# LayerNorm folded into the q and k weights of a gated cross-attention kernel

## The chip, the cores and the metric

The kernel runs on one core of a Trainium2 chip. Its time is the device time of the whole program in microseconds (us). The core has a matrix engine (TensorE, PE in the profile, with its weight loads as PEld), VectorE (DVE), ScalarE (ACT), GpSimd (POOL) and SyncE (SP), which here issues the transfers. Each engine works through its own instructions in order; semaphores tie them together. Lines such as L518 are lines of the kernel before.

## What is computed

The input x is 8 batches of 512 rows by 2048 columns; the context ctx has the same shape. LayerNorm runs along the 2048 columns, so each batch has one mean and one reciprocal deviation for each of its 512 rows.

```python
x = x + tanh(g_xattn) * xattn(layernorm(x), ctx, mask, ...)
x = x + tanh(g_ffn)   * ffn(layernorm(x), ...)

# xattn, on patches of 128 columns, 8 heads of 32 rows
q = Wq @ qk + bq          # Wq, Wk: 256 x 512; qk = layernorm(x)
k = Wk @ qk + bk
val = Wv @ ctx + bv
o = softmax(q^T k / sqrt(32), masked) applied to val
out = (Wo @ gelu(o) + bo) * mask

# ffn, on x as 4 streams of 512 columns
H = sinkhorn(50 iterations on a 4 x 4 matrix per row, from x_norm @ W_res)
out = H mixed over the streams + (H_pre-weighted sum @ W_branch) spread by H_post
```

## The kernel before

The work is cut into 32 blocks of 512 columns, four to a batch, and each block into four steps t, one for each patch of 128 columns. A block of x is held as four tiles of 128 rows by 512 columns (xt). The pool of these tiles has 16 buffers, four blocks.

For block n, `proj(n)` makes q and k. POOL normalizes each of the four tiles (xn, L500), ACT casts it to float16 (xh, L505), and POOL takes the rest as a second float16 tile (xl, L507). The 512 output rows, q and k together, come in four groups m of 128. For each m and each tile, TensorE adds three float16 products in PSUM (L518 to L520): high weights by high x, high weights by low x, low weights by high x. ACT adds the bias and writes the float16 high part (ev, L522), and DVE the low part (L523). SP sends both to a scratch tensor (qd), from where `stack` fetches them into the layout QS and KS of the attention products.

A batch's mean and reciprocal deviation come from `stats(b)`, some blocks earlier: products of transposed x with the ffn weights (lgx, L448; rawp, L467), then squares of x on ACT (xs, L481), then `finish_stats`.

The rest of a step: `vproj` projects the context (vp, L559, float32), `smax` and `expo` form the scores twice (L569, L595), `attv` applies them (u, L612 and L616), and `outp` makes the output rows once per block: POOL multiplies by the mask (o, L632), TensorE transposes (gTp, L641), and four groups of products (op, L667 to L670) are added into xt by DVE (L671). SP stores xt to a scratch tensor (x1s, L674). After a batch, `ffn` runs the Sinkhorn iterations as a chain of small DVE instructions (L844 to L854), and `mixv` mixes the streams (w, L946 and L949 on DVE, L925 and L944 on POOL). Part of the mixing is done by TensorE at the end (`mixp`, L1000 and L1001).

What is emitted in a step follows the string `ORDER`, one letter for one kind of work; a scheduler with a simulated timeline then fixes the order on each engine. During block n, `proj(n + 2)` is run in parts, and in its last step the tiles of x for block n + 3 are requested:

```python
if LXP == 4 and p == 3 and n > 0 and n + 3 < NTOT:
    defer(D_LX, "lx", lambda n=n: load_x(n + 3))
```

The PSUM pool `ps_p`, with two buffers, serves proj, vproj and outp; `ps_t`, with two, serves most small products.

Of the kernel before, what the change touches and what calls it, by code (L numbers as in the profile page):

```python
# [9 lines left out]
F32 = mybir.dt.float32  # L10
# [9 lines left out]
P = 128  # L20
# [5 lines left out]
BLK = 512  # L26
# [9 lines left out]
CT_ACT = False  # L36
MH_ACT = False
XS_ACT = False
LXP = 4
POOLMIX = lambda i, j: j == 1 and i > 0  # L40
BUF_GP = 1
BUF_OP = 1
BUF_XHP = 5
BUF_XNP = 2
BUF_XTP = 4
BUF_CTP = 2
BUF_QDP = 3
# [17 lines left out]
BUF_XPRE = 1  # L65
PSTEPS = (0,1,1,2)
SP0 = 1
XH_POOL = lambda c: False
CAP = 1.0
NORM0 = True  # L70
D_MH = 0
# [1 line left out]
D_X1 = 0  # L73
D_OUT = 0
D_ST = 0
D_LX = 0
CT_PRE = False
BUF_XP = 16
PE_MIX = ((), (), (), (), (3,), (0, 1, 2, 3), (0, 1, 2, 3), (1, 2, 3))
SPLITS = (1, 1, 1, 1, 1, 1, 1, 1)  # L80
CHAINS = ((0,), (1,), (2,), (3,), (4,), (5,), (6,), (7,))
# [18 lines left out]
def gated_xattn_mhc_kernel(  # L100
# [43 lines left out]
    onesb = ctile([P, P], F32, "onesb")  # L144
    V.memset(onesb, 1.0)

    WqkH = ctile([P, 4, 512], F16, "WqkH")
    WqkL = ctile([P, 4, 512], F16, "WqkL")
# [25 lines left out]
    mrow_d = dram.tile([6, B * S], BF16, tag="mrow_d", name="mrow_d")  # L174
    mneg_d = dram.tile([1, B * S], F16, tag="mneg_d", name="mneg_d")
    brow_d = dram.tile([3, 512], F32, tag="brow_d", name="brow_d")


    QS = [ctile([99, NH, SB], F16, f"QS{i}") for i in range(NS)]
# [6 lines left out]
    xnp = ctx.enter_context(tc.tile_pool(name="xnp", bufs=BUF_XNP))  # L186
# [32 lines left out]
    rawx = {}  # L219
    nmean = {}  # L220
    rstd1 = {}
    nb1 = {}
    sq2 = {}
    x1s = {}
    G4 = {}
# [24 lines left out]

    def finish_stats(b, nm, var):
        r = rsqrt(ln0, var, eps_ln, 4, "ln1")
        nb = ln0.tile([P, 4], F32, tag="nb1", name="nb1")
        V.tensor_tensor(nb, nm, r, ALU.mult)
        nmean[b], rstd1[b], nb1[b] = nm, r, nb

    with tc.tile_pool(name="set", bufs=1) as st:

# [66 lines left out]
        for t in range(2):  # L325
            sl = slice(256 * t, 256 * t + 256)
            V.tensor_scalar(wq[:, :, sl], wq[:, :, sl], al[:, t : t + 1], None, ALU.mult)
        A.copy(WqkH, wq)
        V.tensor_tensor(WqkL, wq, WqkH, ALU.subtract)
        for t in range(2):  # L330
            V.tensor_scalar(bqs[:, 2 * t : 2 * t + 2], bcol[:, 2 * t : 2 * t + 2], al[:, t : t + 1], None, ALU.mult)

# [10 lines left out]
        var0 = stile([P, 4], F32, "var0")  # L343
        V.tensor_copy(var0, mv[:, :, 1])
        finish_stats(0, nm, var0)


        mh = stile([B * 16, 3, P], BF16, "mh")
# [91 lines left out]
    def stats(b):  # L440

        lgs = xsp.tile([P, 512], F32, tag="lgs", name="lgs", bufs=1)
        for q4 in range(5):
            if q4 > 0:
                flush(lambda e: e[2] == "st")
                lg = ps_t.tile([P, 512], F32, tag="t", name="lgx")
                for g in range(4):
                    T.matmul(lg[32 * g : 32 * g + 32, :], Wm[:, 4 * q4 - 4 + g, :], xts[g], start=True, stop=True)  # L448
                if q4 == 1:
                    V.tensor_copy(lgs, lg)  # L450
                else:
                    V.tensor_tensor(lgs, lg, lgs, ALU.add)
# [12 lines left out]
        rp = ps_t.tile([P, 4, 32], F32, tag="t", name="rawp")  # L465
        for c in range(4):
            T.matmul(rp[:, c, :], lgs[:, c * P : (c + 1) * P], sel, start=True, stop=True)  # L467
        rw = lnp.tile([P, 4, 32], F32, tag="rawx", name="rawx")
        V.tensor_copy(rw, rp)
        rawx[b] = rw  # L470
        if b == 0:
            return
        nm = ln0.tile([P, 4], F32, tag="nmean", name="nmean")
        V.tensor_scalar(nm, rw[:, :, NM], -1.0 / S, None, ALU.mult)
        yield 1
        sq = lnp.tile([P, 4, NBLK], F32, tag="sq1", name="sq1")
        for c in range(4):
            for k in range(NBLK):
                xs = xtp.tile([P, BLK], F32, tag="xTt", name="xs")
# [12 lines left out]
    def proj(n):  # L492

        b, k = divmod(n, NBLK)
        flush(lambda e: e[2] == "lx")
        xt = xtile[n]
        hs, ls = [], []
        for c in range(4):
            xn = xnp.tile([P, BLK], F32, tag="xn", name="xn")
            G.tensor_scalar(xn, xt[c], rstd1[b][:, c : c + 1], nb1[b][:, c : c + 1], ALU.mult, ALU.add)  # L500
            h = xhp.tile([P, BLK], F16, tag="xh", name="xh")
            if XH_POOL(c):
                G.tensor_copy(h, xn)
            else:
                A.copy(h, xn)  # L505
            l = xhp.tile([P, BLK], F16, tag="xl", name="xl")
            G.tensor_tensor(l, xn, h, ALU.subtract)  # L507
            hs.append(h)
            ls.append(l)
        if NORM0:  # L510
            yield
        qd = qdp.tile([2, 4, 2, P, BLK], F16, tag="qd", name="qd")
        qds[n] = qd
        for m in range(4):
            ps = ps_p.tile([P, BLK], F32, tag="p", name="qk")
            ms = slice(m * P, (m + 1) * P)
            for c in range(4):
                T.matmul(ps, WqkH[:, c, ms], hs[c], start=(c == 0), stop=False)  # L518
                T.matmul(ps, WqkH[:, c, ms], ls[c], start=False, stop=False)  # L519
                T.matmul(ps, WqkL[:, c, ms], hs[c], start=False, stop=(c == 3))  # L520
            ev = evp.tile([P, 2, BLK], F16, tag="ev", name="ev")
            A.activation(ev[:, 0, :], ps, AF.Identity, bias=bqs[:, m : m + 1])  # L522
            V.scalar_tensor_tensor(ev[:, 1, :], ps, bqs[:, m : m + 1], ev[:, 0, :], ALU.add, ALU.subtract)  # L523
            defer(D_QD, "qd", lambda m=m, ev=ev: SY.dma_start(qd[m // 2, 0:2, m % 2].rearrange("t p s -> p t s"), ev))
            yield

    def stack(m):
# [484 lines left out]
            pass  # L1012

    run(proj(0))
    stack(0)
    vproj(0)
    for t in range(2):
# [29 lines left out]
    def act(c, t):  # L1047
# [18 lines left out]
            if p == 2:  # L1066
                at("stack", stack, NSB * (n + 1) + 1)
        elif c == "l" and live_:
            if LXP == 4 and p == 3 and n > 0 and n + 3 < NTOT:
                defer(D_LX, "lx", lambda n=n: load_x(n + 3))  # L1070
            if LXP == 5 and p == 2 and n > 0 and n + 3 < NTOT:
                defer(D_LX, "lx", lambda n=n: load_x(n + 3))
            if p == LXP and n > 1 and n + 2 < NTOT:
                defer(D_LX, "lx", lambda n=n: load_x(n + 2))
# [121 lines left out]
```

## Time and profile before

| | |
|---|---|
| median of 3 runs | 1835.11 us (1830.48 to 1844.21) |
| profiled execution, its own time | 1828.05 us |
| its span, first to last instruction | 1825.9 us |
| busy: PE / PEld / DVE / ACT / POOL | 1547 / 901 / 1382 / 1069 / 603 us |
| mean granted TensorE clock | 0.932 of full speed |
| bytes moved | 331 MB, 181 GB/s over the span |

A line of a group reads: line, engine, operation, output and inputs by the program's names, shapes, count, then busy time in us and the mean ns of one, then the idle time of the engine just before, with what ended it. In the waits, the three numbers are the total in us, how often, and the longest. A line of one source line's instructions gives minimum, median and maximum in ns. Matmuls are pipelined, and the ends shown for them are modelled: they overlap, and two starts lie closer together than one duration.

### The profile page before, as it was taken

The numbers are of one execution on the slowest core, as the hardware profiler recorded it, in microseconds if no ns is written. First come the engines' busy times: TensorE is split into PE (matmuls) and PEld (weight loads), VectorE is DVE, ScalarE is ACT, GpSimd is POOL, SyncE is SP. The second block draws the span as 40 slices with busy tenths as digits, with TensorE's granted clock in tenths as the row PEclk, the third lists the DMA queues.
The fourth block names the chain that finished last, engine by engine and source line by source line (L and its number), as shares of the span: only waits on it lengthen the run. The fifth ranks groups of instructions, "written<-read, shape, count | busy, mean of one in ns | idle before, by whom it ended". The sixth has DMA issues, their size and how long they took to land.

```text
span 1825.9 us, 32268 instructions
## 1 busy us (share of the span) xinstructions
PE 1547.1 (85%) x10517; PEld 901.0 (49%) x10517; DVE 1382.3 (76%) x4201; ACT 1069.4 (59%) x2030; POOL 602.8 (33%) x511
## 2 busy tenths in 40 slices
PE   3998999989889888889878888799888889768887
PEld 2554555555555554545544445455455555543333
DVE  7434345877888778888888879889898998998761
ACT  2386466646555656558565475566665566755454
POOL 0512222322232243342444333444334442321121
PEclk7999999999999988999988999899999999989999
DMA  6478696467646855568555784468755565523443
GB/s 214 139 209 256 208 258 194 140 174 232 180 134 200 254 169 165 151 192 269 162 154 164 214 251 144 139 196 259 215 154 165 148 189 147 172 93 119 144 157 117
DMA packets 353237, 330.60 MB, mean 181 GB/s; under 512 B 53351, under 2 KB 251303, under 8 KB 353070
## 3 DMA queue, kind: packets, MB, share of 16 engines
q1 hardware_dynamic: 353070, 328.55, 60.6%
q8 instruction: 83, 1.36, 0.3%
q14 instruction: 84, 0.69, 0.1%
HBM read 226.71 MB, written 101.16 MB: 180 GB/s over the span
## 4 chain that ended last, share of the span: by engine, by line
PE 37%; DVE 23%; DMA 18%; issue 9%; ACT 9%; POOL 4%; SPq 1%; ACTq 0%; POOLq 0%; DVEq 0%
PE vp L559 5%; DVE w L946 4%; DMA xs<-in_x_dram 4%; PE qk L518 3%; PE qk L519 3%; DMA out_dram<-w 3%; PE qk L520 3%; DMA x<-x1s 2%; PE mx L1000 2%; DMA x1s<-xt 2%; PE lgx L448 2%; DVE mx L571 2%; PE op L667 2%; DVE W L844 2%; PE mx L1001 2%
## 5 line engine op out<-in xcount | busy, mean ns | idle before, releaser
L559 PE MATMUL vp<-Wv,ct 128*128 128x256 f32 x1024 | 272.4, 418 | 16.7 <-DMA ct<-in_cx_dram 15.1
L500 POOL TENSOR_SCALAR xn<-xt,ln_r,nb 128x512 f32<-128x512 f32 x128 | 105.5, 826 | 501.2 <-DMA xt<-in_x_dram 385.7
L559 PEld LDWEIGHTS vp<-Wv,ct 128*128 128x128 f32 x1024 | 207.4, 210 | 68.0 <-issue 18.6
L518 PE MATMUL qk<-xh,WqkH 128*128 128x512 f16 x512 | 199.2, 390 | 29.4 <-ACT xh L505 16.3
L946 DVE SCALAR_TENSOR_TENSOR w<-x,Et,w 128x512 f32<-128x512 f32 x180 | 180.0, 1001 | 49.6 <-POOL w L944 34.0
L519 PE MATMUL qk<-xl,WqkH 128*128 128x512 f16 x512 | 197.9, 387 | 4.3 <-POOL xl L507 4.0
L520 PE MATMUL qk<-xh,WqkL 128*128 128x512 f16 x512 | 197.6, 386 | 0.0
L571 DVE TENSOR_REDUCE mx<-smax 128x8 f32<-128x1024 f32 x128 | 154.9, 1210 | 41.7 <-PE smax L569 41.3
L507 POOL TENSOR_TENSOR xl<-xn,xh 128x512 f16<-128x512 f32 x128 | 156.3, 1228 | 76.0 <-ACT xh L505 70.4
L597 ACT ACTIVATE e<-sT,ebi,esc 128x1024 f32<-128x1024 f32 x128 | 153.4, 1198 | 18.0 <-PE sT L595 17.9
L523 DVE SCALAR_TENSOR_TENSOR ev<-qk,bqs,ev 128x512 f16<-128x512 f32 x128 | 94.5, 739 | 77.5 <-ACT ev L522 76.1
L667 PE MATMUL op<-gh,WoH 128*128 128x512 f32 x256 | 120.9, 474 | 35.3 <-DVE ev L523 31.1
L944 POOL TENSOR_TENSOR w<-w,pj 128x512 f32<-128x512 f32 x60 | 80.1, 1334 | 213.1 <-ACT w L939 113.7
L505 ACT CAST xh<-xn 128x512 f16<-128x512 f32 x128 | 78.3, 612 | 103.7 <-POOL xn L500 102.9
L522 ACT ACTIVATE ev<-qk,bqs 128x512 f16<-128x512 f32 x128 | 86.9, 679 | 85.0 <-PE qk L520 78.7
L673 ACT ACTIVATE junk<-xt,nmean 128x512 bf16<-128x512 f32 x128 | 91.6, 716 | 73.9 <-DVE xt L671 41.3
L850 DVE TENSOR_TENSOR W<-E,uv 128x64 f32<-128x64 f32 x392 | 119.4, 307 | 5.4
L844 DVE TENSOR_TENSOR W<-E,uv 128x64 f32<-128x64 f32 x352 | 117.1, 335 | 4.8
L612 PE MATMUL u<-e,onesb 128*32 128x256 f32 x1024 | 102.7, 403 | 10.5 <-DVE mq L573 3.8
L668 PE MATMUL op<-gl,WoH 128*128 128x512 f32 x256 | 107.1, 418 | 0.0
L669 PE MATMUL op<-gh,WoL 128*128 128x512 f32 x256 | 106.6, 417 | 0.0
L632 POOL TENSOR_TENSOR o<-o,mb 128x1024 f32<-128x1024 f32 x32 | 75.6, 2364 | 93.2 <-ACT o L627 85.9
(287 smaller groups left out, 3504.6 us busy)
## 6 DMA issues: line engine op xcount, KB each, us to landing
xt<-in_x_dram SPq DMA_DIRECT2D x128, 256.0 KB
ct<-in_cx_dram SPq DMA_DIRECT2D x128, 256.0 KB
xTt<-in_xT_dram SPq DMA_DIRECT2D x128, 256.0 KB
qd<-ev SPq DMA_DIRECT2D x128, 256.0 KB
x1s<-xt SPq DMA_DIRECT2D x128, 256.0 KB
xs<-in_x_dram SPq DMA_DIRECT2D x112, 256.0 KB
QS<-qd SPq DMA_DIRECT2D x192, 128.0 KB
KS<-qd SPq DMA_DIRECT2D x192, 128.0 KB
```

The lines of the kernel that those rows point to most:

```text
L507: G.tensor_tensor(l, xn, h, ALU.subtract)
L518: T.matmul(ps, WqkH[:, c, ms], hs[c], start=(c == 0), stop=False)
L519: T.matmul(ps, WqkH[:, c, ms], ls[c], start=False, stop=False)
L520: T.matmul(ps, WqkL[:, c, ms], hs[c], start=False, stop=(c == 3))
L559: T.matmul(ps[:, h, :], ct[:, c, :], Wv[:, c, :], start=(c == 0), stop=(c == 3))
L571: V.tensor_reduce(mx, sc, AX.X, ALU.max)
L597: A.activation(e32, sc, AF.Exp, bias=ebi[:, t : t + 1], scale=esc[:, t : t + 1])
L667: T.matmul(ps, WoH[:, e, cs], gh[:, e], start=(e == 0), stop=False)
L668: T.matmul(ps, WoH[:, e, cs], gl[:, e], start=False, stop=False)
L844: V.tensor_tensor(W4[:, h], E4[:, h], vb[:, h], ALU.mult)
L850: V.tensor_tensor(W4[:, h], E4[:, h], ub[:, h], ALU.mult)
L946: V.scalar_tensor_tensor(w, x1[j], E[:, n, 4 * j + i : 4 * j + i + 1], w, ALU.mult, ALU.add)
```

## The change

The normalization of x goes out of `proj`. The weights of q and k, scaled as before, are kept in float32 in a scratch tensor (wqk_d). For each batch and each m, the new function `weights` loads 128 of their columns, multiplies the rows by the batch's reciprocal deviation on POOL, and makes the bias of q or k from the product of these weights with the negative mean. `proj` then multiplies x itself, in float32, by these weights: four matmuls for each m. Weights for m = 0 and 1 of a batch are made at the end of its `stats`, those for m = 2 and 3 in the projection of the last block of the batch before. The pool of x has 20 buffers in place of 16, and block n + 4 is requested where block n + 3 was.

```diff
-BUF_XHP = 5
-BUF_XNP = 2
+BUF_XHP = 1
+BUF_WQ = 6
-BUF_XP = 16
+BUF_XP = 20
...
     def finish_stats(b, nm, var):
         r = rsqrt(ln0, var, eps_ln, 4, "ln1")
-        nb = ln0.tile([P, 4], F32, tag="nb1", name="nb1")
-        V.tensor_tensor(nb, nm, r, ALU.mult)
-        nmean[b], rstd1[b], nb1[b] = nm, r, nb
+        nmean[b], rstd1[b] = nm, r
+
+    def weights(b, m, src=None):
+        w = wqp.tile([P, 4, P], F32, tag="wq", name="wqb")
+        if src is None:
+            SY.dma_start(w, wqk_d[m])
+            src = w
+        for c in range(4):
+            G.tensor_scalar(w[:, c], src[:, c], rstd1[b][:, c : c + 1], None, ALU.mult)
+        bp = ps_t.tile([P, BLK], F32, tag="t", name="bp")[:, 0:1]
+        for c in range(4):
+            T.matmul(bp, w[:, c], nmean[b][:, c : c + 1], start=(c == 0), stop=(c == 3))
+        bi = ln0.tile([P, 1], F32, tag=f"bi{m}", name="bi")
+        V.tensor_tensor(bi, bp, bqs[:, m : m + 1], ALU.add)
+        wqb[b, m] = (w, bi)
...
-        A.copy(WqkH, wq)
-        V.tensor_tensor(WqkL, wq, WqkH, ALU.subtract)
+        for m in range(4):
+            SY.dma_start(wqk_d[m], wq[:, :, m * P : (m + 1) * P])
...
         finish_stats(0, nm, var0)
+        for m in range(4):
+            weights(0, m, wq[:, :, m * P : (m + 1) * P])
...
         finish_stats(b, nm, var)
+        for m in range(2):
+            weights(b, m)
...
     def proj(n):
         b, k = divmod(n, NBLK)
-        flush(lambda e: e[2] == "lx")
         xt = xtile[n]
-        hs, ls = [], []
-        for c in range(4):
-            xn = xnp.tile([P, BLK], F32, tag="xn", name="xn")
-            G.tensor_scalar(xn, xt[c], rstd1[b][:, c : c + 1], nb1[b][:, c : c + 1], ALU.mult, ALU.add)
-            h = xhp.tile([P, BLK], F16, tag="xh", name="xh")
...
-                A.copy(h, xn)
-            l = xhp.tile([P, BLK], F16, tag="xl", name="xl")
-            G.tensor_tensor(l, xn, h, ALU.subtract)
...
         for m in range(4):
             ps = ps_p.tile([P, BLK], F32, tag="p", name="qk")
-            ms = slice(m * P, (m + 1) * P)
+            if (b, m) not in wqb:
+                weights(b, m)
+            w, bi = wqb[b, m]
             for c in range(4):
-                T.matmul(ps, WqkH[:, c, ms], hs[c], start=(c == 0), stop=False)
-                T.matmul(ps, WqkH[:, c, ms], ls[c], start=False, stop=False)
-                T.matmul(ps, WqkL[:, c, ms], hs[c], start=False, stop=(c == 3))
+                T.matmul(ps, w[:, c], xt[c], start=(c == 0), stop=(c == 3))
             ev = evp.tile([P, 2, BLK], F16, tag="ev", name="ev")
-            A.activation(ev[:, 0, :], ps, AF.Identity, bias=bqs[:, m : m + 1])
-            V.scalar_tensor_tensor(ev[:, 1, :], ps, bqs[:, m : m + 1], ev[:, 0, :], ALU.add, ALU.subtract)
+            A.activation(ev[:, 0, :], ps, AF.Identity, bias=bi)
+            V.scalar_tensor_tensor(ev[:, 1, :], ps, bi, ev[:, 0, :], ALU.add, ALU.subtract)
             defer(D_QD, "qd", ...)
+            if k == NBLK - 1 and m < 2 and (b + 1, 1) in wqb:
+                weights(b + 1, m + 2)
             yield
...
     run(proj(0))
+    load_x(NBLK)
...
-            if LXP == 4 and p == 3 and n > 0 and n + 3 < NTOT:
-                defer(D_LX, "lx", lambda n=n: load_x(n + 3))
+            if p == 3 and n > 0 and n + 4 < NTOT:
+                load_x(n + 4)
```

More of the change, by code (lines that the diff above doesn't have):

```diff
@@ L38 @@
 XS_ACT = False
-LXP = 4
 POOLMIX = lambda i, j: j == 1 and i > 0
@@ L67 @@
 SP0 = 1
-XH_POOL = lambda c: False
 CAP = 1.0
@@ L75 @@
 D_ST = 0
-D_LX = 0
 CT_PRE = False
-BUF_XP = 16
+BUF_XP = 20
 PE_MIX = ((), (), (), (), (3,), (0, 1, 2, 3), (0, 1, 2, 3), (1, 2, 3))
@@ L145, in gated_xattn_mhc_kernel @@
     V.memset(onesb, 1.0)
-    WqkH = ctile([P, 4, 512], F16, "WqkH")
-    WqkL = ctile([P, 4, 512], F16, "WqkL")
     Wv = ctile([P, 4, DK], F32, "Wv")
@@ L176, in gated_xattn_mhc_kernel @@
     brow_d = dram.tile([3, 512], F32, tag="brow_d", name="brow_d")
+    wqk_d = dram.tile([4, P, 4, P], F32, tag="wqk_d", name="wqk_d")
     QS = [ctile([99, NH, SB], F16, f"QS{i}") for i in range(NS)]
@@ L185, in gated_xattn_mhc_kernel @@
     xsp = ctx.enter_context(tc.tile_pool(name="xsp", bufs=2))
-    xnp = ctx.enter_context(tc.tile_pool(name="xnp", bufs=BUF_XNP))
+    wqp = ctx.enter_context(tc.tile_pool(name="wqp", bufs=BUF_WQ))
     xhp = ctx.enter_context(tc.tile_pool(name="xhp", bufs=BUF_XHP))
@@ L221, in gated_xattn_mhc_kernel @@
     rstd1 = {}
-    nb1 = {}
+    wqb = {}
     sq2 = {}
@@ L494, in proj @@
         b, k = divmod(n, NBLK)
-        flush(lambda e: e[2] == "lx")
         xt = xtile[n]
-        hs, ls = [], []
-        for c in range(4):
-            xn = xnp.tile([P, BLK], F32, tag="xn", name="xn")
-            G.tensor_scalar(xn, xt[c], rstd1[b][:, c : c + 1], nb1[b][:, c : c + 1], ALU.mult, ALU.add)
-            h = xhp.tile([P, BLK], F16, tag="xh", name="xh")
[L502 to L505, printed above, removed]
-            l = xhp.tile([P, BLK], F16, tag="xl", name="xl")
-            G.tensor_tensor(l, xn, h, ALU.subtract)
-            hs.append(h)
-            ls.append(l)
         if NORM0:
@@ L1068, in act @@
         elif c == "l" and live_:
-            if LXP == 4 and p == 3 and n > 0 and n + 3 < NTOT:
-                defer(D_LX, "lx", lambda n=n: load_x(n + 3))
[L1071 to L1074, printed above, removed]
+            if p == 3 and n > 0 and n + 4 < NTOT:
+                load_x(n + 4)
         elif c == "s" and live_ and t + AHEAD < NT_:
```

## The prediction

> **What bounds the kernel now.** I read the page's busy shares first, then the table by stage, then the order of single matmuls on TensorE.
>
> ```profile
> PE 1547.1 (85%) x10517; PEld 901.0 (49%) x10517; DVE 1382.3 (76%) x4201; ACT 1069.4 (59%) x2030; POOL 602.8 (33%) x511
> ```
> PE has the largest share, but an average hides stages. The table by stage (columns: length, then busy time of PE, PEld, DVE, ACT, POOL, the granted TensorE clock, DMA share, GB/s) separates them:
>
> ```profile
> 60.00:350.00 290.00, 268.89 (x2001) 159.26 (x1999) 131.05 (x296) 177.55 (x336) 85.97 (x76) 0.98 0.73 212
> 350.00:650.00 300.00, 271.04 (x2051) 165.82 (x2052) 244.55 (x759) 176.62 (x360) 86.85 (x77) 0.97 0.65 193
> 650.00:950.00 300.00, 245.91 (x1704) 149.80 (x1704) 247.86 (x702) 182.13 (x348) 121.81 (x97) 0.91 0.63 184
> 950.00:1250.00 300.00, 252.69 (x1791) 149.21 (x1791) 253.69 (x728) 176.34 (x334) 109.70 (x90) 0.90 0.61 183
> 1250.00:1550.00 300.00, 258.33 (x1863) 159.98 (x1862) 267.18 (x801) 193.32 (x370) 128.39 (x104) 0.93 0.62 181
> ```
> Up to 650 us PE is busy 93% and 90%: this stage is TensorE's. From 650 us on, PE (82 to 86%) and DVE (83 to 89%) share the limit, and the clock is lower. The chain that ended last agrees that no engine rules alone:
>
> ```profile
> PE 37%; DVE 23%; DMA 18%; issue 9%; ACT 9%; POOL 4%; SPq 1%; ACTq 0%; POOLq 0%; DVEq 0%
> ```
> A block (512 columns of one batch; 32 of them) takes about 48 us: some 1540 us from 60 to 1600, divided by 32. The last 226 us hold no projection and are left alone by the change.
>
> **PE: the projection.** The timeline of PE shows the price of both forms side by side (start, duration, instruction):
>
> ```profile
> 63.74 3.62 PE L559 MATMUL vp<-Wv,ct 128*128 128x256 f32 x16
> 67.19 0.38 PE L518 MATMUL qk<-xh,WqkH 128*128 128x512 f16 x1
> 67.41 0.38 PE L519 MATMUL qk<-xl,WqkH 128*128 128x512 f16 x1
> 67.62 0.38 PE L520 MATMUL qk<-xh,WqkL 128*128 128x512 f16 x1
> ```
> Durations (0.38) overlap, so I take distances between starts. Float16: 0.215 us for 512 columns. Float32: the 16 records are 8 matmuls (two records each) of 256 columns and take 67.19 - 63.74 = 3.45 us, 0.431 each, so 0.862 for 512 columns: four times float16. One m of the projection was 12 float16 matmuls, 12 x 0.2155 = 2.59 us, and becomes 4 float32 ones, 4 x 0.862 = 3.45 us. With 32 blocks x 4 m = 128: 331 us become 442 us, **+110 us**. Fewer instructions, more time.
>
> Here a rule speaks differently. The Trainium skill, Perfetto Trace Analysis, "Identifying the Most-Contended Engine", calls matmul busy time a bad measure of TensorE and points to the busy share of weight loads instead (with FLOP utilization). That share is 49%, and the change moves it little: 1536 float16 loads x 0.099 = 152 us go, 1024 x 0.19 = 195 us of float32 loads come. By that rule half of TensorE is free and the +110 us cost nearly nothing; by the distances above the array is occupied without a gap inside each group, and they cost in full wherever PE sets the pace. I take the distances.
>
> **PE: the bias products.** 32 calls (4 m x 8 batches) of 4 float32 matmuls with one column, each with a full float32 weight load. Nearest row, the same load with 32 columns, 8 groups of 4:
>
> ```profile
> L467 PE MATMUL rawp<-sel,lgs 128*128 128x32 f32 x64 | 9.4, 288 | 4.1 <-DVE lgs L452 4.1
> ```
> 9.4 / 8 = 1.18 us per group, **+38 us**. Lower end 0.6 us per call (half of the loads hidden under the matmul before): 19 us. Upper end: PE is in order and waits for POOL's scaling, which may stand behind one 2.4 us POOL operation (o L632, gl L657): 3 us more for each of 28 calls, +84; queued behind on PE are smax, sT and u. It also borrows one of the two PSUM buffers of "t". The products of a batch are issued about a block ahead of their use, so I take 38.
>
> **POOL and ACT.** Removed per block: 4 xn, 4 xl, 4 xh.
>
> ```profile
> L500 POOL TENSOR_SCALAR xn<-xt,ln_r,nb 128x512 f32<-128x512 f32 x128 | 105.5, 826 | 501.2 <-DMA xt<-in_x_dram 385.7 <-DVE nb L254 71.3 <-DVE W L844 20.2
> L507 POOL TENSOR_TENSOR xl<-xn,xh 128x512 f16<-128x512 f32 x128 | 156.3, 1228 | 76.0 <-ACT xh L505 70.4 <-DVE mq L573 1.4 <-DVE W L850 1.2
> L505 ACT CAST xh<-xn 128x512 f16<-128x512 f32 x128 | 78.3, 612 | 103.7 <-POOL xn L500 102.9
> ```
> 262 us of POOL and 78 us of ACT go. Added on POOL: 128 scalings of 128x128; between the 0.21 us of a 128x4 copy (L635) and the 0.77 median of L500, by width 0.35 us, 45 us in all. POOL falls from 603 to 386 us. Neither engine is a bound, so the direct gain is only what PE waited for.
>
> ```profile
> PE op L667 <- DVE ev L523: 31.1, 21, 4.9
> ...
> PE qk L518 <- ACT xh L505: 16.3, 13, 4.7
> ...
> PE qk L518 <- DVE ev L523: 10.7, 7, 3.6
> ...
> PE qk L519 <- POOL xl L507: 4.0, 7, 1.3
> ```
> The waits for xh and xl, 20 us, go with their producers. The two for ev are waits for a PSUM buffer of the projection to be emptied by ACT and DVE (0.68 + 0.74 us); with 3.45 instead of 2.59 us of matmuls between two of them, I take half, 21 us. Together **-41 us** (ends -20 and -62). What is late next is the same DVE eviction, and DVE's gT (18 us), which stay.
>
> **DVE behind POOL.** The second rule, and it speaks for the change: SBUF — State Buffer, "Who interferes with whom", says that a VectorE instruction with two SBUF inputs and a GpSimd instruction that reads SBUF exclude each other, the later one blocking fully. The trace agrees in kind:
>
> ```profile
> L946 DVE SCALAR_TENSOR_TENSOR w<-x,Et,w x180: 647/746/2962, 510.4 to 1821.4; 128x512 f32<-128x512 f32 x180
> L850 DVE TENSOR_TENSOR W<-E,uv x392: 154/224/2371, 329.1 to 1766.4; 128x64 f32<-128x64 f32 x196
> ```
> Mean minus median, times count: L946 (1001-746) x 180 = 46 us; L850 33; L844 39; mq L573 and L574 32; L860 and L861 7: 157 us of blocked DVE. POOL loses 36% of its work, so 56 us of it. Read as a bound by the rule, DVE and the time gain 56; by the chain, of which DVE is 23%, 13 (below nothing there is no reason to go: nothing is added to DVE but 32 tiny adds). DVE is a co-limit in the later stage, so I take **-20**.
>
> **Clock.** Later stages are granted 0.90 to 0.93, the first 0.98. Fewer gaps on PE may raise it: at most 5% of 757 us of PE work, 38; lower end 0; I take **-10**.
>
> **x tiles and queues.** load_x(n+4) stands where load_x(n+3) stood. With 20 tiles it reuses block n-1's, as before with 16: SP still waits for that block's x1s store (104 us in total, 76 times), so SP is not freed; x merely arrives a block earlier. POOL's 386 us of waiting for xt cost nothing, as POOL was idle; what reached PE is in the 16.3 us already. SP gets 32 more transfers (4 stores, 28 loads of 256 KB, some 0.45 us of issue each) under 1540 us of body; bytes rise by 8.4 MB on 331. The loads of m = 2, 3 wait for a weight buffer that PE is still reading: at most 3.45 us x 14 = 48 us of SP standing, with ct, qd and QS/KS behind it; I take 0, as those loads are issued ahead. Without that cover it costs the 48. In the prologue wbr, which shares wq's space, now waits for the 16 scalings (about 43 to 48 us instead of 41), and PE for its product; PE then has 14 us of proj(0) to do. The first matmul comes 1 or 2 us earlier, proj(0) lasts 3.5 us longer: 0 to +4, I take 0.
>
> **Sum** against the profiled execution (span 1825.9, time 1828.05): +110 +38 -41 -20 -10 = +77, so **1905 us**. By stage: 60 to 650 us is 12.3 blocks x 4.6 = +57, less some 11 us of these waits there, +46; the rest, 19.7 blocks, +91 less 60, +31. The median of the runs shown is 1835, 7 us above the profiled one, within their spread (1830 to 1844); a difference under 1% cannot be told from none.
>
> **Rivals.**
> (a) Faster: the pair that DVE and POOL share decides. If from 650 us on DVE alone sets the pace, PE's added 91 us fit in its gaps there (143 us in 900), and DVE loses its whole 56 us, plus the 41 us of PE waits. 46 - 56 - 10 leaves about 1808. For it: DVE at 89% beside PE at 86%. Against it: the first 590 us lose whatever happens later, and DVE is 23% of the chain. It decides only if the later stage gains over 46 us. Chance 0.10.
> (b) No credit: PE is the bound throughout and other waits take the place of those removed: 1828 + 148 = 1976. For it: waits on PE are spread over many small causes. Chance 0.20.
> (c) The new waits decide: bias products behind POOL and SP standing for weight buffers, +77 + 84/2 + 48/2 = 1971. Chance 0.08; indistinguishable from (b) by time, not by the waits.
> (d) The later stage absorbs its share, the earlier pays: 1828 + 46 = 1874 or somewhat less. Chance 0.17.
> (e) It does not do what it says: x arrives no earlier because SP is blocked as before. The change then still pays for PE; it adds to (b).
> My forecast, 1905 within about 25, has the remaining 0.45. Within 1% of before: 0.06, taken from the near side of (a) and (d). Slower by over 1%: 0.85; faster by over 1%: 0.09. The range leaves out (a) and half of (b): 1850 to 1972.
>
> **What would show it.** The profile after should have distances of 0.86 us between starts of the new qk matmuls and about 440 us for them; PE busy near 90% or more in every stage up to the end of the projections; POOL near 390 us; L946 nearer to 0.9 us mean; no wait of PE for xh. Wrong if the new matmuls stand closer than 0.8 us, if the stage up to 650 us gets no longer, or if PE's waits grow by more than the 41 us removed.

## The result and the profile after

The kernel became slower. Its median is 1937.51 us (1926.71 to 1940.55, four runs); the kernel before, on the same chip, 1833.38 us (four runs). The ratio is 1.0546 [1.0484, 1.0608], some +104 us. The profiled execution took 1940.55 us, its span is 1938.8 us: 113 us more than the span of before, where +77 was forecast. Below, lines of the changed kernel have its own numbers: the new matmul is L521, the scaling L259, the bias product L262; L949 is the former L946, L635 the former L632.

The page's busy shares of the changed kernel:

```profile
PE 1664.9 (86%) x10197; PEld 976.6 (50%) x10261; DVE 1376.4 (71%) x4224; ACT 1001.3 (52%) x1901; POOL 415.7 (21%) x383
```
PE is busy 118 us longer (1547.1 before). PE without work is span less busy time: 1825.9 - 1547.1 = 279 us before, 1938.8 - 1664.9 = 274 us after. So the 113 us are more work on TensorE, and little idle time was won for it. One thing has to be read first: PE shows 10197 records and its weight loads 10261. 64 matmul records are missing from this trace, all of one row, which is shown here before and after:

```profile
L670 PE MATMUL op<-MR,bo 128*128 128x512 bf16 x128 | 53.0, 414 | 0.0
L673 PE MATMUL op<-MR,bo 128*128 128x512 bf16 x64 | 25.4, 397 | 0.0
```
Most of a missing record's time is covered by the modelled end of its neighbour. In the five traces that have all 128 (before, e1 to e4), leaving out every second record of this row lowers PE's busy time by 6 to 9 us; so about 7 us of work stand here as idle. With them, TensorE works +125 us (1672 in all) and idles 12 us less (267). Traces below with the same gap of 63 to 65 between the two counts are corrected by the same 7 us, and the text says so.

The table by stage, columns as before:

```profile
60.00:350.00 290.00, 269.88 (x1720) 161.26 (x1730) 107.04 (x224) 141.74 (x267) 42.09 (x47) 0.96 0.72 207
350.00:650.00 300.00, 275.86 (x1856) 167.30 (x1862) 229.88 (x758) 147.43 (x298) 44.78 (x40) 0.96 0.58 167
650.00:950.00 300.00, 255.40 (x1595) 152.94 (x1605) 229.82 (x643) 164.99 (x323) 72.70 (x63) 0.93 0.66 191
950.00:1250.00 300.00, 260.46 (x1651) 160.23 (x1661) 250.99 (x767) 167.43 (x320) 87.92 (x79) 0.94 0.64 186
1250.00:1550.00 300.00, 252.33 (x1632) 155.97 (x1643) 236.45 (x679) 159.83 (x304) 78.73 (x67) 0.91 0.58 168
```
From 650 to 1550 us PE is busy 768 of 900 us, 85%, where it was 757, 84%. The forecast wanted 90% there. DVE falls from 769 to 717 us in this stretch, but fewer blocks pass in it: by the starts of POOL's mask multiply (L635), 15.7 where 17.0 passed before. A block costs PE 48.8 us instead of 44.4, and DVE 45.6 instead of 45.1. The price on PE is there almost whole (4.6 us per block were forecast), and DVE has no less to do per block.

The single matmuls on PE's timeline (start, duration, instruction):

```profile
57.06 0.95 PE L262 MATMUL bp<-nmean,wqb 128*128 128x1 f32 x8
57.87 0.83 PE L418 MATMUL ws<-Wm,onesb 128*128 128x32 f32 x6
58.54 3.68 PE L521 MATMUL qk<-xt,wqb 128*128 128x512 f32 x8
62.06 1.20 PE L418 MATMUL ws<-Wm,onesb 128*128 128x32 f32 x10
```
Four new matmuls (eight records) take 62.06 - 58.54 = 3.52 us, 0.88 each, beside the 0.862 forecast. Four bias products take 57.87 - 57.06 = 0.81 us. (Over the whole trace, from the first start of such a group to the next matmul, where no other product comes between: 3.54 and 0.87 us in the median.)

The costliest groups that the change adds or touches:

```profile
L521 PE MATMUL qk<-xt,wqb 128*128 128x512 f32 x1024 | 491.3, 618 | 24.3 <-DVE ev L524 14.6 <-ACT VF L563 9.7
L262 PE MATMUL bp<-nmean,wqb 128*128 128x1 f32 x256 | 34.4, 244 | 4.0 <-POOL wqb L259 3.5 <-DVE g4s L651 0.4
L259 POOL TENSOR_SCALAR wqb<-wqb,ln_r 128x128 f32<-128x128 f32 x112 | 68.1, 625 | 132.7 <-DVE ln_r L244 82.2 <-DMA wqb<-wqk_d 50.4
L949 DVE SCALAR_TENSOR_TENSOR w<-x,Et,w 128x512 f32<-128x512 f32 x180 | 156.6, 870 | 45.0 <-ACT w L942 20.7 <-POOL w L947 15.1 <-DMA x<-x1s 8.9
```
PE waits for neither xh nor xl any more, as those are gone. Its listed waits nonetheless total 262 us, against 269 before. The first seven lines are of the changed kernel, the last two of the kernel before:

```profile
PE gTp L644 <- POOL o L635: 30.6, 10, 7.0
PE smax L572 <- ACT mh L581: 25.7, 12, 4.3
PE vp L562 <- DMA ct<-in_cx_dram: 25.1, 12, 5.7
PE op L670 <- DVE ev L524: 19.1, 11, 3.4
PE qk L521 <- DVE ev L524: 14.6, 3, 12.3
PE vp L562 <- DVE ev L524: 7.6, 3, 5.9
PE g L648 <- DVE gT L645: 11.0, 8, 2.6
PE smax L569 <- ACT mh L578: 7.4, 4, 2.5
PE vp L559 <- DMA ct<-in_cx_dram: 15.1, 16, 2.2
```
op's wait for ev eased from 31.1 to 19.1, g's for gT from 18.1 to 11.0. But all waits for ev together stay as they were, 41.8 before and 41.3 now: vp waits for it too, and one wait of qk, 12.3 us, lies in the prologue at 51.5 us. And others grew: smax for mh from 7.4 to 25.7, vp for ct from 15.1 to 25.1, and one wait of vp for KS of 7.7.

The chain that ended last, of this one execution:

```profile
PE 38%; DMA 19%; DVE 17%; ACT 10%; issue 6%; SPq 2%; POOL 2%; another core or an unknown queue 0%; ACTq 0%; POOLq 0%; DVEq 0%
```
DVE had 23% of it and has 17%: it did lose weight. PE's own share (37 to 38%) and that of the transfers (18 to 19%) hardly grew.

SP's queue, for the request of x (L229 is the transfer in `load_x`; before it was L233 with 103.6 us, 76 times):

```profile
SPq L229 <- DMA x1s<-xt: 90.6, 59, 3.9
```
With the four tiles more, SP stands as before for the store of an older block.

### The profile page after: what moved, and what is told of

It reads as the page before. It is cut to its first block, busy times and chain, and to the rows that moved or that the text cites. A ratio compares the mean times of both kernels' runs of the same rounds, so it can differ in the third digit from the quotient of the medians.

```text
span 1938.8 us, 31533 instructions
## 1 busy us (share of the span) xinstructions
PE 1664.9 (86%) x10197; PEld 976.6 (50%) x10261; DVE 1376.4 (71%) x4224; ACT 1001.3 (52%) x1901; POOL 415.7 (21%) x383
## 4 chain that ended last, share of the span: by engine, by line
PE 38%; DMA 19%; DVE 17%; ACT 10%; issue 6%; SPq 2%; POOL 2%; another core or an unknown queue 0%; ACTq 0%; POOLq 0%; DVEq 0%
PE qk L521 9%; DMA x<-x1s 4%; PE vp L562 4%; DMA xs<-in_x_dram 4%; DMA out_dram<-w 3%; DMA ct<-in_cx_dram 3%; DVE w L949 2%; PE op L670 2%; PE lgx L460 2%; PE mx L1003 2%; DVE W L853 2%; PE mx L1004 2%; PE op L671 2%; DVE mx L574 2%; PE op L672 2%
## 5 line engine op out<-in xcount | busy, mean ns | idle before, releaser
L521 PE MATMUL qk<-xt,wqb 128*128 128x512 f32 x1024 | 491.3, 618 | 24.3 <-DVE ev L524 14.6
L562 PE MATMUL vp<-Wv,ct 128*128 128x256 f32 x1024 | 268.7, 414 | 44.4 <-DMA ct<-in_cx_dram 25.1
L521 PEld LDWEIGHTS qk<-xt,wqb 128*128 128x128 f32 x1024 | 189.4, 196 | 219.1 <-issue 186.2
L949 DVE SCALAR_TENSOR_TENSOR w<-x,Et,w 128x512 f32<-128x512 f32 x180 | 156.6, 870 | 45.0 <-ACT w L942 20.7
L523 ACT ACTIVATE ev<-qk,bi 128x512 f16<-128x512 f32 x128 | 86.9, 679 | 172.1 <-PE qk L521 167.8
L635 POOL TENSOR_TENSOR o<-o,mb 128x1024 f32<-128x1024 f32 x32 | 75.7, 2366 | 404.8 <-ACT o L630 338.2
L524 DVE SCALAR_TENSOR_TENSOR ev<-qk,bi,ev 128x512 f16<-128x512 f32 x128 | 94.0, 734 | 89.1 <-ACT ev L523 86.3
L670 PE MATMUL op<-gh,WoH 128*128 128x512 f32 x256 | 123.1, 482 | 20.3 <-DVE ev L524 19.1
L572 PE MATMUL smax<-KS,QS 97*128 97x128 f16 x1024 | 85.8, 226 | 38.2 <-ACT mh L581 25.7
L674 DVE TENSOR_TENSOR xt<-op,xt 128x512 f32<-128x512 f32 x128 | 87.2, 681 | 41.0 <-remote 19.9
L493 ACT ACTIVATE xs<-xs,nmean 128x512 f32<-128x512 f32 x112 | 79.9, 715 | 66.4 <-DMA xs<-in_x_dram 50.0
L928 POOL TENSOR_TENSOR xpre<-xpre,pj 128x512 f32<-128x512 f32 x57 | 74.0, 1298 | 158.3 <-ACT pj L927 147.1
L621 ACT ACTIVATE rc<-u 128x256 f32<-128x256 f32 x128 | 47.8, 373 | 116.4 <-PE u L619 79.7
L855 DVE TENSOR_REDUCE sm<-W 128x16 f32<-128x64 f32 x392 | 101.6, 259 | 8.1
```

The lines of the kernel that those rows point to most:

```text
L521: T.matmul(ps, w[:, c], xt[c], start=(c == 0), stop=(c == 3))
L524: V.scalar_tensor_tensor(ev[:, 1, :], ps, bi, ev[:, 0, :], ALU.add, ALU.subtract)
L562: T.matmul(ps[:, h, :], ct[:, c, :], Wv[:, c, :], start=(c == 0), stop=(c == 3))
L670: T.matmul(ps, WoH[:, e, cs], gh[:, e], start=(e == 0), stop=False)
L855: V.tensor_reduce(sm[:, h], W4[:, h].rearrange("p n i j -> p n j i"), AX.X, ALU.add)
L949: V.scalar_tensor_tensor(w, x1[j], E[:, n, 4 * j + i : 4 * j + i + 1], w, ALU.mult, ALU.add)
```

## The experiments

Three theories stood against each other. T1: TensorE's own time is the price, and it is paid in full wherever it falls. T2: the work taken from POOL and ACT gives a part of it back. T3: the credits were lost to new waits (bias products behind POOL, SP behind the stores, x late). Ratios are against the kernel before on the same chip, whose medians were 1838.52 us for e1 to e4, 1834.43 for e5 to e8 and 1833.06 for e9 to e12; differences in us across these groups carry some 5 us of that.

**e1, the price alone.** The kernel before with a fourth float16 product for each tile; nothing else changes.

```diff
-                T.matmul(ps, WqkL[:, c, ms], hs[c], start=False, stop=(c == 3))
+                T.matmul(ps, WqkL[:, c, ms], hs[c], start=False, stop=False)
+                T.matmul(ps, WqkL[:, c, ms], ls[c], start=False, stop=(c == 3))
```


> The kernel before with the fourth float16 product, low weights by low x, added: 16 float16 matmuls for each m, 16 x 0.2155 = 3.45 us, the same TensorE time as four float32 matmuls. POOL, ACT, x tiles and waits stay as before. If the TensorE price is the main cause: 110 us added, less some 20 us of ev waits, 1833 + 90 = about 1920. If the later stage hides TensorE work and the loss of the change comes from bias products and weight waits: under 1880.

1955.58 us, ratio 1.0649 [1.0612, 1.0687], +117 us. The added time on TensorE is 512 x 0.2155 = 110 us, the same as the forecast gave the float32 projection. It is paid in full: nothing of it went into gaps, and the 20 us that its expectation took off for ev waits did not come either. Op's and qk's waits for ev did fall, from 41.8 to 29.8 us, but PE's idle time is 281 us beside 279: vp for ct (15.1 to 24.7) and smax for mq (7.3 to 16.3) took the place. Its busy shares:

```profile
PE 1673.9 (86%) x11029; PEld 957.4 (49%) x11029; DVE 1433.0 (73%) x4201; ACT 1073.6 (55%) x2030; POOL 603.0 (31%) x511
```
The share of weight loads is 49% as it was before. By that share half of TensorE was free, by the distances between starts 110 us cost 110. The distances were right. The page that the prediction names asks for the FLOP utilization beside the share of weight loads, and that was not worked out; e1 speaks of the share alone.

**e2, sixteen tiles.** The changed kernel with the old pool of x and the old request. Everything else of the fold stays.

```diff
-BUF_XP = 20
+BUF_XP = 16
...
-    load_x(NBLK)
...
-            if p == 3 and n > 0 and n + 4 < NTOT:
-                load_x(n + 4)
+            if p == 3 and n > 0 and n + 3 < NTOT:
+                load_x(n + 3)
```


> The changed kernel with 16 x tiles and block n + 3 requested, as before. By the prediction the earlier load only gives slack: within 10 us of the changed kernel, 1930 to 1945. If the earlier x is what removed waits: TensorE waits for xt at L521, 15 to 40 us more, 1955 to 1980.

1920.29 us, 1.0458 [1.042, 1.0497]: 17 us faster than the changed kernel, not slower. And this although a wait appears on PE that the early request had removed:

```profile
PE qk L521 <- DMA xt<-in_x_dram: 50.0, 28, 4.9
```
50 us of waiting for x came and the time fell: the early request did bring x earlier, but bought no time. The 17 us are within what e12 below shows for the order alone.

**e3, no bias products.** Left out: the products of the weights with the mean and their addition; the bias is that of before.

```diff
-        for c in range(4):
-            T.matmul(bp, w[:, c], nmean[b][:, c : c + 1], start=(c == 0), stop=(c == 3))
-        bi = ln0.tile([P, 1], F32, tag=f"bi{m}", name="bi")
-        V.tensor_tensor(bi, bp, bqs[:, m : m + 1], ALU.add)
-        wqb[b, m] = (w, bi)
+        wqb[b, m] = (w, bqs[:, m : m + 1])
```


> The changed kernel without the bias products: the part of the bias that comes from the mean is left out, the bias is the constant one. By the prediction's term 38 us less: about 1900. If the weight loads of these products hide under other matmuls: 10 to 20 us less, about 1922. If waits for POOL's scaling cost on top: 50 us or more less, under 1890.

1875.98 us, 1.023 [1.0178, 1.0283], -61 us. The products themselves are 32 x 0.81 = 26 us. The rest could be waits behind POOL, or order; e5 and e10 bear on that.

**e4, POOL's work kept.** The changed kernel with eight operations on 128x512 per block on POOL whose results nobody reads, in place of xn and xl.

```diff
+        for c in range(4):
+            xn = xhp.tile([P, BLK], F32, tag="xn", name="xn")
+            G.tensor_scalar(xn, xt[c], rstd1[b][:, c : c + 1], nmean[b][:, c : c + 1], ALU.mult, ALU.add)
+            xl = xhp.tile([P, BLK], F16, tag="xl", name="xl")
+            G.tensor_tensor(xl, xn, xt[c], ALU.subtract)
```


> The changed kernel with POOL's normalization and subtraction put back for every x tile, their results unused: 262 us of POOL work return, nothing waits for it. If freeing DVE from POOL is worth the predicted 20 us: about 1957, with L949 back near 1000 ns mean. If it is worth the whole 56 us of DVE: about 1990. If nothing: 1937.

1965.72 us, 1.0708 [1.0661, 1.0755], +28 us on the changed kernel. The page of e4, then its group of the mixing:

```profile
PE 1685.1 (86%) x10261; PEld 981.3 (50%) x10261; DVE 1456.0 (74%) x4224; ACT 1002.0 (51%) x1901; POOL 698.5 (36%) x639
```

```profile
L954 DVE SCALAR_TENSOR_TENSOR w<-x,Et,w 128x512 f32<-128x512 f32 x180 | 171.0, 950 | 39.3 <-POOL w L952 24.4 <-DMA x<-x1s 10.7 <-ACT w L947 3.5
```
DVE has no instruction more, and is busy 80 us longer for 283 us of work on POOL: 0.28 us per us. The mean of the mixing instruction goes from 870 to 950 ns, but that of one group proves little: over the 14 traces it is 825 to 933 where POOL is busy 416 to 423 us, and 891 to 1001 where it is busy 603 or more. DVE's busy total separates them better: 1361 to 1384 us in the eight traces with the small POOL load, 1382 to 1433 in the five with 603 to 610 (before, e1, e8, e9, e11), 1456 here with 698. So more work on POOL goes with a longer DVE, as the second rule has it. The size is uncertain: the changed kernel itself, with 187 us less on POOL, has only 6 us less on DVE than before, and e1, with POOL as before, 51 more. Of the 80 us some 28 reached the end, give or take the order (e12).

**e5, bias products twice.** Each group of four is issued twice, and the second overwrites the first.

```diff
-        for c in range(4):
-            T.matmul(bp, ...)
+        for _ in range(2):
+            for c in range(4):
+                T.matmul(bp, ...)
```


> The changed kernel with each group of bias products made twice into the same PSUM tile, the second overwriting the first. The trace after shows 0.81 us for a group of four, 26 us for 32. If their cost is TensorE time: 26 us more, about 1963. If it is mostly their order, the PSUM buffer and the chain to the bias (61 us came off without them): under 10 us more, as none of these is added.

1936.68 us, 1.0576 [1.0544, 1.0608]: the time of the changed kernel, with 26 us more of TensorE. The page of e5:

```profile
PE 1686.4 (88%) x10454; PEld 1001.3 (52%) x10517; DVE 1378.3 (72%) x4224; ACT 1002.9 (52%) x1901; POOL 419.9 (22%) x383
```
PE's busy time did rise (by 21 us, with 63 records missing where the changed kernel misses 64), and its idle time fell, from 267 to 228 us. So with e3, one group of these products is worth 61 us when it is taken away and nothing when it is added. A price of an instruction cannot do that; something else moves at each edit.

**e6, ACT's casts kept.** Four casts per block whose results nobody reads.

```diff
+        for c in range(4):
+            h = xhp.tile([P, BLK], F16, tag="xh", name="xh")
+            A.copy(h, xt[c])
```


> The changed kernel with ACT's casts of the x tiles put back, their results unused: 78 us of ACT work. If the relief of ACT is the larger part of what the change gives back (four products cost 117, the changed kernel without bias products only 38): 20 to 45 us more, about 1970. If ACT was never late and the waits for xh were the point: within 8 us of 1938.

1957.42 us, 1.0672 [1.0615, 1.0729], +20 us on the changed kernel, with ACT at 1070 us. Same sign as e4, and no larger than the effect of order (e12).

**e7, twenty tiles, the request three blocks on.** The changed kernel with its 20 tiles, but block n + 3 requested as before: the tiles that it reuses are those of block n - 2.

```diff
-    load_x(NBLK)
...
-            if p == 3 and n > 0 and n + 4 < NTOT:
-                load_x(n + 4)
+            if p == 3 and n > 0 and n + 3 < NTOT:
+                load_x(n + 3)
```


> The changed kernel with its 20 x tiles, but block n + 3 requested: the tile to be reused was stored a block earlier, so SP should not stand for the x1s store. If SP's standing (91 us in 59 waits) holds up other loads: below the 16-tile kernel's 1920, about 1905. If not: 1915 to 1925. If the 20 tiles themselves are what cost: about 1937.

1885.01 us, 1.0279 [1.026, 1.0297]: 52 us faster than the changed kernel, 35 faster than e2, from which it differs by the number of tiles alone. The page of e7, then its SP queue and its clock:

```profile
PE 1648.3 (88%) x10198; PEld 965.4 (51%) x10261; DVE 1381.8 (73%) x4224; ACT 1001.1 (53%) x1901; POOL 418.5 (22%) x383
```

```profile
SPq L229 <- DMA x1s<-xt: 48.9, 31, 3.4
```

```profile
core 0: 1882.7 us, clock 0.948
```
SP stands 49 us instead of 85 in e2 (91 in the changed kernel). With the missing records put back (7 us), PE is busy 1655 us and idle 227; e2, with none missing, 1679 and 239. So 11 us of the gain are idle time and 24 are busy time. The second part goes with the clock, 0.948 instead of 0.938 (over the four executions of each, 0.946 to 0.948 beside 0.933 to 0.945). In these traces the granted clock is either full or half: the new matmuls start 0.429 us apart (per record) in the stretches of full clock of the changed kernel and 0.854 in those of half. PE was busy 184 us in half-clock stretches in e2 and 147 in e7; half of the difference, 18 us, is what that cost.

**e8, the fold in float16.** e2, but x and the folded weights are split into float16 high and low parts and multiplied in three products, as before. This takes the float32 price away and leaves the fold. (Not shown: the float32 weights have two buffers here, and xh and xl five again.)

```diff
+        wh = wqp.tile([P, 4, P], F16, tag="wh", name="wh")
+        A.copy(wh, w)
+        wl = wqp.tile([P, 4, P], F16, tag="wl", name="wl")
+        G.tensor_tensor(wl, w, wh, ALU.subtract)
...
+            A.copy(h, xt[c])
...
+            G.tensor_tensor(l, xt[c], h, ALU.subtract)
...
-                T.matmul(ps, w[:, c], xt[c], start=(c == 0), stop=(c == 3))
+                T.matmul(ps, wh[:, c], hs[c], start=(c == 0), stop=False)
+                T.matmul(ps, wh[:, c], ls[c], start=False, stop=False)
+                T.matmul(ps, wl[:, c], hs[c], start=False, stop=(c == 3))
```


> LayerNorm folded into the weights, but the projection in three float16 products: x is split by ACT (high) and POOL (low) as it comes, the folded weights are split once per batch and m; 16 tiles, block n + 3. POOL's normalization (105 us) is gone, the bias products stay. From the 16-tile kernel's 1920: 110 us less for TensorE, some 16 more for POOL's subtraction and 20 for ACT's casts: about 1845. If folding itself is worth something where TensorE pays nothing for it: under 1825.

1910.79 us, 1.0408 [1.0348, 1.0468]: 10 us below e2, and still 76 above the kernel before. 110 us of TensorE were taken away and 10 came back. So the fold loses without its float32 price as well; e11 and the part after e12 show where.

**e9, the kernel before with twenty tiles.** One constant; no fold.

```diff
-BUF_XP = 16
+BUF_XP = 20
```


> The kernel before with 20 x tiles in place of 16, block n + 3 requested as before, nothing else: a tile is asked for one block after its store instead of right behind it. If SP's standing for the x1s store (104 us before) costs here what it cost in the changed kernel (52 us between four blocks on and three blocks on): about 1785, faster than both. If the 52 us belong to the changed kernel only: 1825 to 1840.

1800.66 us, 0.9831 [0.9783, 0.988]: faster than both kernels, by 32 us than before. The page of e9, then its SP queue:

```profile
PE 1528.8 (84%) x10453; PEld 898.4 (50%) x10517; DVE 1393.9 (77%) x4201; ACT 1068.7 (59%) x2030; POOL 606.0 (33%) x511
```

```profile
SPq L233 <- DMA x1s<-xt: 26.0, 23, 3.5
```
SP's standing for the stores falls from 104 us to 26. All engines do the work of before. With the 64 missing records (7 us), PE is busy 1536 us instead of 1547 and idle 274 instead of 279, so PE's waits show little of the gain: vp's wait for ct even rises from 15 to 35 us.

**e10, e7 without bias products.** The edit of e3 on e7.

```diff
-        wqb[b, m] = (w, bi)
+        wqb[b, m] = (w, bqs[:, m : m + 1])
```


> 20 tiles, block n + 3 requested, and the bias products left out (the mean's part of the bias is missing). If the two gains are separate: 1885 - 61 = about 1824. If the 61 us of the bias products were largely another order of the other work and the same loading trouble: 1850 to 1880.

1856.87 us, 1.0155 [1.0101, 1.0209]: 28 us below e7, about the 26 us of the products themselves, where the same edit had been worth 61 on the changed kernel.

**e11, e8 with twenty tiles.**

```diff
-BUF_XP = 16
+BUF_XP = 20
```


> The float16 fold with 20 tiles, block n + 3 requested. Against the float32 fold in the same loading (1885) it has 110 us less of TensorE work, and POOL's subtractions and ACT's casts again (some 16 and 20 us by the runs that kept them). If the TensorE price is what rules: about 1815. If, as with 16 tiles (1911 against 1920), the chain from x over ACT and POOL to the products takes it back: 1865 or more.

1891.66 us, 1.032 [1.0279, 1.036]: 19 us below e8, and 7 above e7, which does the same in float32. The page of e11, and its clock:

```profile
PE 1599.3 (84%) x10709; PEld 956.1 (50%) x10773; DVE 1415.1 (75%) x4224; ACT 1084.7 (57%) x2061; POOL 604.3 (32%) x543
```

```profile
core 0: 1895.5 us, clock 0.910
```
e7 was granted 0.948. PE was busy 268 us in half-clock stretches here and 147 in e7; half of the difference is 61 us, and so busy time (1606 with the missing records) falls by only 49 us from e7's 1655, where 110 fewer were to be done. Idle time rises by 62 at once, from 227 to 289. A lower clock and new idle time took what was saved.

**e12, the order alone.** The changed kernel with the four bias products of a group in the reverse order. The work is the same to the last instruction, but the scheduler lays all engines out anew.

```diff
-        for c in range(4):
-            T.matmul(bp, ..., start=(c == 0), stop=(c == 3))
+        for c in (3, 2, 1, 0):
+            T.matmul(bp, ..., start=(c == 3), stop=(c == 0))
```


> The changed kernel with the four bias products of a group in reversed order: the same work, but the scheduler lays out all engines anew. If the order it finds is worth tens of us by itself: more than 15 us away from 1938, either way. If the sizes above are those of the edits: 1928 to 1948.

1913.85 us, 1.0437 [1.0405, 1.047]: 24 us below the median of the changed kernel, for no work less. Its page shows the same work, 1 record apart:

```profile
PE 1660.9 (87%) x10198; PEld 967.1 (50%) x10261; DVE 1382.3 (72%) x4224; ACT 1000.0 (52%) x1901; POOL 417.9 (22%) x383
```
This is the scale on which every edit here has to be read. It comes from one reordering, and can be larger: the edit of e3 was worth 61 us on one layout and 28 on another (e10). The +117 of e1 stands far above it. e2 (-17), e4 (+28) and e6 (+20) are of its size: their signs are what T2 expects, their sizes are not settled. The bias products lie between nothing (e5) and 61 us (e3), their own 26 us in the middle.

**All traces side by side.** One profiled execution each, in us, with 7 us put back where records are missing, ordered by PE's idle time. Where nothing else is said, a fold has 20 tiles and the request four blocks on, a kernel without it 16 and three:

| kernel | span | PE busy | PE idle | clock |
|---|---|---|---|---|
| e10 fold, no bias products, 20 tiles, three on | 1851 | 1627 | 224 | 0.945 |
| e7 fold, 20 tiles, three on | 1883 | 1655 | 227 | 0.948 |
| e5 fold, bias products twice | 1921 | 1693 | 228 | 0.942 |
| e2 fold, 16 tiles, three on | 1918 | 1679 | 239 | 0.938 |
| e3 fold, no bias products | 1874 | 1632 | 242 | 0.942 |
| e12 fold, other order | 1915 | 1668 | 247 | 0.940 |
| the changed kernel | 1939 | 1672 | 267 | 0.934 |
| e6 fold, ACT's casts kept | 1950 | 1680 | 270 | 0.933 |
| e9 before, 20 tiles | 1810 | 1536 | 274 | 0.936 |
| e4 fold, POOL's work kept | 1963 | 1685 | 278 | 0.934 |
| before | 1826 | 1547 | 279 | 0.932 |
| e1 before, four products | 1955 | 1674 | 281 | 0.929 |
| e11 float16 fold, 20 tiles, three on | 1896 | 1606 | 289 | 0.910 |
| e8 float16 fold, 16 tiles, three on | 1893 | 1588 | 305 | 0.919 |

This is what T2 needed. Seven layouts of the float32 fold idle 224 to 267 us, the kernels without the fold 274 to 281, and the fold with POOL's or ACT's work kept 270 and 278. So taking that work away does give idle time back, some 40 us by the means of these groups (239, 274 and 278 us for fold, work kept and no fold), and the changed kernel is the one of the seven that got least of it. The middle group is two layouts only, and beside the changed kernel alone they idle just 3 and 11 us more. Of T3, the changed kernel shows 3.5 us of waiting behind POOL's scaling and no wait of PE for x; for SP there are only the pairs below.

Two pairs compare the fold with the kernel before at equal tiles and equal request. Before to e2 is +82 us by medians, e9 to e7 +84. On PE these are 132 and 119 us more busy time, 40 and 46 less idle time. Beside them, the changed kernel's +104 holds some 20 us that the fold alone does not cost; the same work in the order of e12 does not have them either (+81).

What no single pair shows, several do. Twenty tiles against sixteen, each time with the request three blocks on, gained 35 us (e2 to e7), 19 (e8 to e11) and 32 (before to e9). The request three blocks on instead of four, with twenty tiles, gained 52 (to e7) and 19 (e3 to e10). Five pairs, each laid out anew, and one sign. SP's standing for the stores fell in each of them: 85 to 49 us, 73 to 39, 104 to 26, 91 to 49, 82 to 68. That this is the way by which the time fell is argued from it, not shown by a chain, and PE's waits do not show it (e9).

## Why the prediction was right, and where its sums were off

The direction and the main mechanism held: the time grew because TensorE's products grew, and no other engine hid them. The size was met only roughly: 1937.51 us lies 32 above the 1905, outside its "within about 25", and 39 below rival (b)'s 1976. The sum was +77 us and the profiled execution shows +113. Step by step:

- **The projection, +110.** 3.52 us instead of 3.45 per four matmuls: 128 x (3.52 - 2.59) = +119. e1 shows on its own that such an addition is paid in full. The rule on weight loads would have said nearly nothing.
- **The bias products, +38.** The group takes 0.81 us between starts and not 1.18: 26 us. The prediction took busy time here, 9.4 us for 8 groups, where it had taken distances for the projection. By busy time L262 itself has 34.4 / 32 = 1.08 us per group, so the nearest row was not too dear, the measure was. The upper end, waits behind POOL, does not appear in this kernel: L262 waited for the scaling 3.5 us in all. Both prices together are +145 by distances, against 148; that is luck, as the two errors cancel. PE's busy total grew by 125, so some 20 of the 145 do not show in it, and it was not traced why.
- **PE's waits, -41.** This is the term that came least. In the changed kernel PE idles 12 us less. The step as put was that the waits for xh and xl "go with their producers" and that half of those for ev go too. The first did go, 20 us; those for ev stayed at 41 in all, and smax's for mh and vp's for ct came. TensorE is in order, and where one wait is gone the next producer is late, as rival (b) said, with a smaller bill. The forecast named DVE's eviction and gT as what is late next: the eviction was, gT eased. But the term is not refuted for the fold as such: in the two pairs of equal tiles and request the idle time fell by 40 and 46 us, in e12 by 32. Which waits go then differs with the layout (e2 has 50 us for x).
- **DVE behind POOL, -20.** The mean of L949 fell to 870 ns (0.9 was forecast), with the same median:

```profile
L949 DVE SCALAR_TENSOR_TENSOR w<-x,Et,w x180: 646/741/2865, 528.0 to 1934.3; 128x512 f32<-128x512 f32 x180
```
By mean less median that is 23 us where it was 46. But the busy total of DVE fell only from 1382 to 1376 us, and PE's share in the later stage stayed at 85%. What the -20 brought can't be told apart from the waits; e4's +28 for more POOL work than was removed fits a few us to 20.

- **Clock, -10.** The profiled executions have 0.934 and 0.932, and PE was busy 186 and 188 us at half clock: nothing. Over all executions the changed kernel has 0.934 to 0.943 and the kernel before 0.922 to 0.934, a rise of nearly 1%. The reason given, fewer gaps on PE, fits the table: the layouts with less idle time have the higher clocks, and this one had little less.
- **By stage.** The twelfth start of L635 is at 662 instead of 605 us, +57, the thirteenth at 746 instead of 677, +69, and the last at 1739 instead of 1624, +115. So 12 blocks cost 57 to 69, where +46 was forecast up to 650 us, and the rest 46 to 58, where +31 was. In the early stage that is the full price (12.3 blocks of 3.7 + 0.8 us, 56 us) and no credit; in the later one the price is 19.7 x 4.5 = 89 us, and 31 to 43 of credit came of the 60 forecast. Of the early +57, 24 fell between the first and the second block: the second starts at 191 us against 164, with no wait of PE over 5 us there. Other work was put before it: 40 records of vp where there were 5, and the next batch's rawp and two groups of its bias products. Without the bias products (e3) it starts at 171.
- **POOL.** 416 us instead of 386: a scaling of 128x128 takes 0.625 us, not 0.35. It did not bound anything.
- **x tiles and queues, 0.** The reading was right ("SP is not freed; x merely arrives a block earlier"), but SP's standing was given no price. The pairs with twenty tiles say that it was worth 19 to 35 us, if it is that by which they gained, and the change spent its four tiles on an earlier request instead.

So the fold as such cost +82 and +84 us where +77 was forecast, and the further 20 or so of the changed kernel belong to its layout or its early request. Which of the two stays open: e7, with the request three blocks on, is 52 us faster, but e12, with the request as in the change, is 24 faster by its order alone. How SP's standing reaches the end of the kernel was not traced inside a block.

Why the fold in float16 loses can be read from the traces. e8's span is 67 us over that of before, 41 of it busy and 26 idle; e11's is 86 over e9's, 70 busy and 15 idle. The bias products are some 21 of the busy time (as much as e5 added). PE was busy at half clock 223 us in e8 beside 188, and 268 in e11 beside 169; half of that is 18 and 49 us. In e8 PE waits for xh 42.0 us (16.3 before), for xl 9.7 (4.0), and the bias products for the scaling 21.0 (14.7 of it once). Why the clock fell stays open.

## What to carry to other kernels

Price work on TensorE by the distance between starts in this program's own timeline; it was paid in full here. Credits for removed waits are real but loose: PE's idle time fell by 12 to 46 us in the float32 fold's layouts compared above, because on an in-order engine another late producer takes the place of the one removed, and which one depends on the layout. When a pool gets more buffers, look at what its refill waits for: the same four tiles were worth nothing as an earlier request and 1.7% with the request left where it was, one constant changed. Where a scheduler lays out all engines, run the same work in another order first, and read no single edit below that difference (24 us here, 1.2%); pairs with one sign say more.

## What was not expected of the hardware

The granted clock goes with PE's idle time, as the table shows: 0.938 to 0.948 in the six kernels that idle 224 to 247 us, 0.929 to 0.936 from 267 to 281, 0.919 at 305. e11 stands below that line, with 0.910 at 289. The two float16 folds are the lowest, 0.910 to 0.921 over eight executions, where the same fold in float32 had 0.933 to 0.948 over eight (e2, e7). The form of the products alone does not set it: before, e1 and e9, float16 as well, have 0.922 to 0.937. Which is cause and which is effect was not tested.

On POOL, a 128x128 scaling of float32 takes 0.602 us in the median where 128x512 took 0.772: with a quarter of the columns, 78% of the time.
